# One step of a masked-attention kernel: another order, smaller TensorE tiles, other release points for the gathers

## The chip, the cores and the metric

The kernel runs on one core of a Trainium2 chip. The metric is the device time of one execution, in microseconds (us). A core has TensorE (PE; its weight loads are listed as PEld), VectorE (DVE), ScalarE (ACT), GpSimd (POOL) and SyncE (SP), each working through its own queue in order; they wait for each other on semaphores. DMA transfers are issued from SP, POOL and ACT queues.

## The reference, cut to what matters

The inputs are `x` (8 batches, 2048 nodes, 64 channels) and an integer adjacency matrix of 2048 by 2048, sparse but for the first nodes. Two graph-attention layers follow, then a leaky ReLU, a layer norm, a residual sum with `x` and a second layer norm. In one layer each node attends only to its neighbours and itself:

```python
def _gat_layer(h, mask, b):
    scores = jnp.einsum('...nd,...md->...nm', h, h)
    scores = jnp.where(mask, scores, NEG)
    attn = jax.nn.softmax(scores, axis=-1)
    return jnp.einsum('...nm,...md->...nd', attn, h) + b
...
h = jnp.einsum('bnc,hdc->bhnd', x, Wh)                      # 4 heads of 64
out_h = _gat_layer(h, mask[None, None], bh[None, :, None, :])
z = jax.nn.leaky_relu(cat, negative_slope=0.2)              # cat: heads side by side
h2 = jnp.einsum('bnk,dk->bnd', z, Wo)
out2 = _gat_layer(h2, mask[None], bo)
```

All of it is float32.

## The kernel before, in words

The first 56 nodes ("hubs") have many neighbours and are treated densely. The other 1992 nodes are split into 166 sets of 12; each set has a list of at most 128 nodes that its members are linked to. The kernel has three parts, all laid out by hand: program order is queue order on each engine.

**Hub stage** (to about 144 us). `x` is loaded, stored as `table1` in device memory, transposed by `turn_x` into `xT`, and the hubs' scores and values are computed. Meanwhile adjacency rows are loaded (`load_adj`, `raw` tiles, three buffers; reduced to 0/1 on GpSimd), turned into keys by small products (`make_keys`) and picked into neighbour lists by VectorE (`pick`, a list of jobs that the loops take one by one with `some`). The sets are listed in three rounds of 60, 60 and 46; only the first is complete when layer 1 starts.

**Layer 1** (to about 600 us) is a loop over `i`, in which one group of two sets passes through per step, each part of a step working on another group. For group `g`:
- `gather` (L792): two indirect DMAs on GpSimd's queue fetch 128 rows of `table1` each into `rows` tiles (ten buffers).
- `turn` (L512): eight TensorE transposes of 128x128 against the identity into the PSUM tile `t`; ScalarE copies `t` to `xTg`.
- `own_rows` (L800, GpSimd): own nodes' columns out of `xT`, into `xo`, every second step for two groups; `columns` (L806): `xo` times the 128x128 matrices `gram`, block diagonal with two copies of Wh^T Wh of a head; ScalarE keeps the product as `y`.
- `scores` (L821): `xTg` against `y`, in tiles of 64x64; `weigh` (L826) subtracts the mask on VectorE, `lift` (L833) is the exponential on ScalarE.
- `values` (L846): exponentials times gathered rows, with the sums of weights in an extra column; `invert` (L853, L854) divides on VectorE.
- `turn_values` (L863): four transposes of the quotients; `keep_values` (L870) copies them to `ot`.
- `project` (L531), `leaky` (L518) and `leak` (L523): the four heads' weights, bias and leaky ReLU.
- `second_maps` (L880): times Wo; `keep_own` (L885, L886) stores the result as `own`; `second_rows` (L890) transposes it, and `keep_rows` (L894) adds the bias and sends it to `table2`.

The PSUM tiles S, C, O and T have one buffer of two banks each. Within step `i` TensorE's order is: scores of group i+1, projection i-1, values i, maps i-2, rows i-3, columns i+4, first half of turn i+3, turned values i, second half of turn i+3. Gathers for group i+5 follow the values in program order; they wait until the values have let go of their buffers. In the first nine steps one more adjacency piece each is loaded and reduced (`more`), and VectorE works off the later rounds' selection jobs. From step 30 on, `load_own` and `add_beta` prepare `table3` (x plus beta) for the end.

**Layer 2** (to the end) starts when `table2` is complete: 42 steps `u` of four sets, with its own order: scores (L1133), values (L1165), transposed exponentials (L1144), `turn2` (which calls `turn`), hub parts (L1277, L1299), and the two norms spread over later steps on VectorE.

## Time and profile before

| | |
|---|---|
| median of 3 runs | 881.2 us (876.9, 881.2, 884.0) |
| the profiled execution | 880.76 us, of it 878.9 from first to last instruction |
| mean granted TensorE clock | 0.951 |

Busy us in stretches (start and end in us):

| stretch | part | length | PE | PEld | DVE | ACT | POOL | clock |
|---|---|---|---|---|---|---|---|---|
| 70 to 144 | hub stage | 74.0 | 54.8 | 37.9 | 57.9 | 24.2 | 21.3 | 0.93 |
| 152.1 to 197.7 | first steps of layer 1 | 45.6 | 39.7 | 34.4 | 27.7 | 24.2 | 21.0 | 0.93 |
| 219.5 to 584.8 | 71 steps of layer 1 | 365.3 | 358.9 | 325.1 | 256.7 | 241.5 | 200.8 | 1.00 |
| 600 to 645 | between the layers | 45.0 | 31.0 | 27.5 | 15.5 | 21.1 | 30.4 | 0.80 |
| 645 to 752 | layer 2 | 107.0 | 104.5 | 96.5 | 93.2 | 87.1 | 82.0 | 1.00 |

A row of a timeline gives start and length in us, engine, line of the kernel, operation, result and operands, the weights' shape on TensorE (rows*columns), result and operand sizes and a count; in brackets the idle time before it and what ended that. Float32 products take two passes on TensorE and are counted twice; transposes are counted once. Matmuls are pipelined, so lengths overlap: the time that a group takes is read from the start of one group to the start of the next.

### The profile page before, as it was taken

The page shows a single profiled execution, that of the slowest core. Times are in us where ns is not written, and L with a number is a line of the kernel's source. Part 1 is how long each engine was busy: PE and PEld are TensorE (multiplying, and loading weights), DVE is VectorE, ACT ScalarE, POOL GpSimd, SP SyncE. Part 2 cuts the span into 40 slices and gives each one's busy share as a digit, 9 for nine tenths or more (in the row PEclk, how much of TensorE's full clock was granted, in tenths as well). Part 3 has the DMA queues.
Part 4 walks back from the last instruction along what each step waited for, and adds up shares of the span by engine and source line. Part 5 has one row for each costly group of instructions (what it writes and reads, how often), then busy time and mean ns, then how long its engine had stood idle before and what let it go on. Part 6 is the DMA issues. An engine that isn't in the chain of part 4 may idle for free.

```text
span 878.9 us, 42066 instructions
## 1 busy us (share of the span) xinstructions
PE 753.0 (86%) x18437; PEld 661.2 (75%) x18437; DVE 610.1 (69%) x1369; ACT 514.4 (59%) x961; POOL 469.2 (53%) x612
## 2 busy tenths in 40 slices
PE   1896777889999999999999999992999999998730
PEld 1664456778788999988999999971899999988720
DVE  3356983568888788877555555553258999998994
ACT  2342333556556667666766667651678888886821
POOL 5654141457444555655666666503777777777300
PEclk9998998999999999999999999995999999999965
DMA  8787451355434445655566665514888888888611
GB/s 167 238 218 213 129 146 48 83 142 160 109 100 118 112 125 159 162 169 153 160 168 173 160 166 162 134 28 114 246 266 253 275 275 267 266 252 242 172 46 35
DMA packets 81794, 145.22 MB, mean 165 GB/s; under 512 B 30146, under 2 KB 46466, under 8 KB 81602
## 3 DMA queue, kind: packets, MB, share of 16 engines
q0 software_dynamic: 26720, 88.55, 36.4%
q1 hardware_dynamic: 37842, 49.65, 18.7%
q10 hardware_dynamic: 17040, 4.25, 2.6%
q8 instruction: 147, 2.41, 1.1%
q14 instruction: 45, 0.37, 0.1%
HBM read 123.91 MB, written 18.48 MB: 162 GB/s over the span
## 4 chain that ended last, share of the span: by engine, by line
PE 63%; DVE 15%; DMA 7%; ACT 5%; issue 4%; SPq 3%; POOL 2%; DVEq 0%; ACTq 0%; POOLq 0%
PE t L512 11%; PE s L821 10%; PE o L846 10%; PE cat L806 6%; PE o L863 4%; PE cat L531 4%; PE cat L880 3%; PE s L1133 3%; PE o L1165 3%; PE cat L890 2%; DMA raw<-in_adj_dram 2%; SPq L1248 2%; PE sh L1277 2%; PE e L1144 2%; DMA g<-table,index 1%
## 5 line engine op out<-in xcount | busy, mean ns | idle before, releaser
L792 POOL DMA_INDIRECT g<-table,index x332 | 334.9, 1009 | 236.1 <-PE o L846 140.2
L512 PE MATMUL t<-ident,g 128*128 128x128 f32 x1328 | 182.3, 276 | 15.6 <-DMA g<-table,index 12.7
L512 PEld LDWEIGHTS t<-ident,g 128*128 128x128 f32 x1328 | 154.8, 142 | 20.0 <-issue 14.0
L826 DVE TENSOR_TENSOR e<-s,mask 128x768 f32<-128x768 f32 x83 | 79.4, 956 | 87.4 <-PE s L821 85.4
L518 ACT ACTIVATE z<-cat,bhp 128x192 f32<-128x192 f32 x166 | 60.8, 418 | 85.0 <-PE cat L531 85.0
L846 PE MATMUL o<-g,e 128*64 128x65 f32 x2656 | 97.5, 227 | 0.0
L821 PEld LDWEIGHTS s<-y,xTg 64*64 64x64 f32 x5312 | 85.2, 134 | 13.9 <-issue 13.7
L821 PE MATMUL s<-y,xTg 64*64 64x48 f32 x5312 | 95.5, 220 | 0.0
L846 PEld LDWEIGHTS o<-g,e 128*64 128x64 f32 x2656 | 85.8, 140 | 9.8
L1320 ACT COPY xTg<-t 128x1024 f32<-128x1024 f32 x83 | 80.3, 1017 | 18.1 <-PE t L512 17.3
L1030 ACT COPY xTg<-t 128x1024 f32<-128x1024 f32 x83 | 84.0, 1012 | 2.0 <-PE t L512 2.0
L833 ACT ACTIVATE e<-e,shifts 128x768 f32<-128x768 f32 x83 | 79.2, 955 | 2.1 <-DVE e L826 1.7
L812 ACT COPY y<-cat 128x384 f32<-128x384 f32 (+1 forms) x80 | 40.7, 508 | 64.0 <-PE o L863 40.1
L597 ACT ACTIVATE e<-e,shifts 128x896 f32<-128x896 f32 x32 | 33.4, 1042 | 73.0 <-DVE e L594 52.1
L680 POOL TENSOR_SCALAR a<-raw 120x1024 bf16<-120x1024 int32 (+1 forms) x34 | 38.2, 1125 | 65.1 <-DMA raw<-in_adj_dram 38.4
L806 PE MATMUL cat<-xo,gram 128*128 128x192 f32 (+1 forms) x320 | 65.6, 328 | 0.0
L853 DVE RECIPROCAL rall<-o 64x8 f32<-64x8 f32 x166 | 34.0, 205 | 42.0 <-PE o L846 40.7
L854 DVE TENSOR_TENSOR osb<-o,rall 128x512 f32<-128x512 f32 x83 | 57.4, 692 | 2.9
L1165 PE MATMUL o<-g,es 128*32 128x65 f32 x2656 | 49.1, 226 | 5.9 <-DVE y_s L1188 4.5
L806 PEld LDWEIGHTS cat<-xo,gram 128*128 128x128 f32 x320 | 53.7, 203 | 0.3 <-issue 0.2
L1165 PEld LDWEIGHTS o<-g,es 128*32 128x32 f32 x2656 | 46.1, 113 | 7.0 <-issue 4.9
L1133 PE MATMUL s<-xTg,bd 128*32 128x128 f32 x1328 | 45.4, 277 | 6.2 <-ACT bd L1124 3.5
(177 smaller groups left out, 1369.3 us busy)
## 6 DMA issues: line engine op xcount, KB each, us to landing
raw<-in_adj_dram SPq DMA_DIRECT2D x32, 480.0 KB
table<-xb SPq DMA_DIRECT2D x22, 256.0 KB
xr_s<-table SPq DMA_DIRECT2D x21, 256.0 KB
g<-table,index POOLq DMA_INDIRECT x332
table<-x SPq DMA_DIRECT2D x16, 260.0 KB
x<-in_x_dram ACTq DMA_DIRECT2D x32, 128.0 KB
table<-rowt SPq DMA_DIRECT2D x166, 24.4 KB
xb<-in_x_dram SPq DMA_DIRECT2D x164, 24.0 KB
```

What stands on the lines that cost most here:

```text
L512: nc.tensor.transpose(tp[:, q * P:(q + 1) * P], rows[:, q, 1:1 + P], ident)
L518: nc.scalar.activation(z[:, hp], cat[:, :, hp * n:(hp + 1) * n], AF.Identity, bias=bhp[:, hp:hp + 1], scale=1.0)
L792: nc.gpsimd.indirect_dma_start(out=t.rearrange("n q c -> n (q c)"), out_offset=None, in_=table, in_offset=bass.IndirectOffsetOnAxis(ap=ind ...
L806: nc.tensor.matmul(cat[:, k, 2 * GM:2 * GM + n], gram[:, g % 2 * 2 + k, :], held["x", g // 2][:, :n], start=True, stop=True)
L821: nc.tensor.matmul(sp[half(r), p, (q * 2 + j) * M:(q * 2 + j + 1) * M], xt[half(p), j, q, half(r)], y[half(p), (j * Q + q) * M:(j * Q + q ...
L826: nc.vector.tensor_tensor(e[:, :16 * M].rearrange("p (a q n) -> p a q n", a=2, q=Q), sp[:, :, :8 * M].rearrange("p a (q n) -> p a q n", q= ...
L833: nc.scalar.activation(e[:, :16 * M], e[:, :16 * M], AF.Exp, bias=shifts[:, 0:1], scale=1.0)
L846: nc.tensor.matmul(op[half(p), j, o0:o0 + K1], e[:, c0:c0 + 64], rw[j][:, q, sums(p)], start=True, stop=True)
L1030: nc.scalar.copy(t, held.pop(("tp", i + 2)))
L1133: nc.tensor.matmul(sp[q * 32:(q + 1) * 32, k, :], bd[u % 3][:, k, q, :], xt[:, s % 2, q, :], start=True, stop=True, tile_position=(0, q * 32))
L1165: nc.tensor.matmul(op[t * 32:(t + 1) * 32, f, k * W2 + p:k * W2 + p + K1], e[:, 2 * q + p, k, :], rw[:, q, sums(p)], start=(a == 0 and k = ...
L1320: nc.scalar.copy(t, tp)
```

## The change

Layer 1's step gets a new order and a longer pipeline, and several products get other tile shapes:

- **Order on TensorE** in step `i`: scores i+1, projection i-2, columns i+4, maps i-3, values i, turned values i-1, rows i-4, turn i+3. The loop has one more pass. The results move to other PSUM tiles: columns beside the values (O), maps into T, turned values and rows into C.
- **Tiles.** A transpose of 128 rows becomes two of 64 rows each (`turn`, in all three parts of the kernel; `second_rows`), and the turned values' four become eight of 48 rows; the two of a pair write different PSUM banks. `columns` uses the two 64x64 blocks of `gram` in four row and column halves of TensorE instead of the block-diagonal matrix. For this, `own_rows` lays the columns out so that half of them swap partition halves: one GpSimd copy becomes three, two of which (new L812) go from one partition half to the other.
- **Gathers.** Four groups ahead instead of five; the first of a pair waits for the end of this step's scores, the second for the middle of this step's values, through dependencies given by hand. `load_adj` stands between them in the steps that have it; the copy into `own` (`store_own`), `own_rows` and `add_beta` stand behind the second.
- **VectorE.** Each selection job is split in two halves, and the counts per step go with it: six in the hub stage and in the steps before 0, three to step 15, then two. The place of `weigh`, `leak`, `invert` and of the jobs in the queue changes with the order above.
- `load_own` and `add_beta` run from step 10 on, two rounds in six steps.
- Layer 2's scores read the turned rows in two pieces of 64, as `turn` lays them out now.

In the built program's order on GpSimd, the first of the two swapping copies waits for the semaphores of all gathers that stand ahead of it in the queue.

```diff
-    def turn(tp, rows):
+    def turn(tp, rows, j=0):
         for q in range(Q):
-            nc.tensor.transpose(tp[:, q * P:(q + 1) * P], rows[:, q, 1:1 + P], ident)
+            c0 = (j * Q + q) * 64
+            for r in range(2):
+                nc.tensor.transpose(tp[:, r, c0:c0 + 64], rows[half(r), q, 1:1 + P], ident[half(r), half(r)])
...
-    def gather(table, s, layer, new):
+    def gather(table, s, layer, new, behind=None):
...
+        if behind is not None:
+            tc.add_manual_dep(g.ins, behind.ins.name, mybir.DependencyInfo(mybir.DependencyClass.Sync, mybir.DependencyReason.DATA),
+                              reason="the gather's turn")
...
     def own_rows(m):
-        w = min(4, NS - 4 * m)
         t = held["x", m] = work.tile([P, 2 * GM], F32, tag="xo", name=f"xo{m}", bufs=2)
-        src = xT[:, :, HUB:].rearrange("c q (k s) -> c s q k", s=NS)[:, 4 * m:4 * m + w]
-        nc.gpsimd.tensor_copy(t[:, :w * 48].rearrange("c (s q k) -> c s q k", s=w, q=Q), src)
+        v = t.rearrange("c (b s q k) -> c b s q k", b=2, s=2, q=Q)
+        src = xT[:, :, HUB:].rearrange("c q (k s) -> c s q k", s=NS)
+        nc.gpsimd.tensor_copy(v[:, 0], src[:, 4 * m:4 * m + 2])
+        b0 = min(4 * m + 2, NS - 2)
+        for r in range(2):
+            nc.gpsimd.tensor_copy(v[half(r), 1], src[half(1 - r), b0:b0 + 2])
-    def columns(g, cat):
-        n = min(4, NS - 4 * (g // 2)) * 48
+    def columns(g, op):
+        t = held["x", g // 2]
         for k in range(2):
-            nc.tensor.matmul(cat[:, k, 2 * GM:2 * GM + n], gram[:, g % 2 * 2 + k, :], held["x", g // 2][:, :n], start=True, stop=True)
+            for r in range(2):
+                for p in range(2):
+                    nc.tensor.matmul(op[half(p), r, Q * OW + k * GM:Q * OW + (k + 1) * GM], gram[half(r), g % 2 * 2 + k, half(r)],
+                                     t[half(r), (p ^ r) * GM:((p ^ r) + 1) * GM], start=True, stop=True)
...
-    def turn_values(g, op):
-        osb = held.pop(("o", g))
+    def turn_values(g, pt):
+        osb = held.pop(("o", g)).rearrange("a j q c -> a (j q c)")
         for w in range(4):
-            nc.tensor.transpose(turned(op)[:, w, :], osb[:112, w].rearrange("a s c -> a (s c)"), ident[:112, :112])
+            for p in range(2):
+                mine = slice(p * 64, p * 64 + M)
+                at = nc.tensor.transpose(pt[:, p, w * M:(w + 1) * M], osb[mine, w * P:(w + 1) * P], ident[mine, mine])
...
-    LOOK = 5
-    for g in range(LOOK - 2):
+    LOOK = 4
+    for g in range(3):
...
-    for i in range(-4, NG + 3):
+    for i in range(-4, NG + 4):
...
+        scored = scores(i + 1, sp) if 0 <= i + 1 < NG else None
...
+        coming = i + LOOK if i > 0 else i + LOOK + 1 if -2 <= i < 0 else NG
+        if coming < NG:
+            gather(table1, 2 * coming, 1, rows_tile, scored)
+        op = one(f"o{i}", "O")
+        if 0 <= i + 4 < NG + NG % 2:
+            columns(i + 4, op)
...
+            more(1)
...
+        if 0 <= i - 3 < NG:
+            second_maps(i - 3, tp[:, 0, :GM])
+            keep_own(i - 3, tp[:, 0, :GM])
+        midway = values(i, op) if 0 <= i < NG else None
+        if coming < NG:
+            gather(table1, 2 * coming + 1, 1, rows_tile, midway)
+        if 0 <= i - 3 < NG:
+            store_own(i - 3)
+        if i + 6 < NG and i % 2 == 0 and i >= -2:
+            own_rows((i + 6) // 2)
...
+        if 0 <= i - 1 < NG:
+            turn_values(i - 1, cat[:, :, 2 * GM:4 * GM])
+        if 0 <= i - 4 < NG:
+            second_rows(i - 4, cat[:GM, :, 384:448])
...
         if 0 <= i + 3 < NG:
-            turn(tp[:, 1, :], rows[1, 2 * (i + 3) + 1])
+            held["tp", i + 3] = tp
+            for j in range(2):
+                turn(tp, rows[1, 2 * (i + 3) + j], j)
```

## The prediction

> **What bounds the kernel now.** I read the busy shares first, then the slices, then stretches of the main stage, then one of its steps instruction by instruction. From the page, section 1 and the TensorE rows of the slices:

> ```profile
> PE 753.0 (86%) x18437; PEld 661.2 (75%) x18437; DVE 610.1 (69%) x1369; ACT 514.4 (59%) x961; POOL 469.2 (53%) x612
> ...
> PE   1896777889999999999999999992999999998730
> ...
> PEclk9998998999999999999999999995999999999965
> ```

> TensorE is full from about 200 to 595 us and again from 640 to 810 us, at the full granted clock. The two stretches (start and end, length, then the busy time of PE, PEld, DVE, ACT and POOL with counts, granted clock, DMA share, GB/s):

> ```profile
> 219.50:584.80 365.30, 358.89 (x9738) 325.08 (x9737) 256.68 (x658) 241.53 (x497) 200.76 (x265) 1.00 0.52 141
> ...
> 645.00:752.00 107.00, 104.51 (x2575) 96.53 (x2574) 93.15 (x165) 87.11 (x153) 82.02 (x83) 1.00 0.87 266
> ```

> The first is layer 1's loop. Its scores start every 4.997 us in most steps; 71 steps take 365.3 us, so 10.5 us of it are extra time in a few steps (the key products, the slot tables). One step on TensorE, by start and length:

> ```profile
> 485.35 1.15 PE L821 MATMUL s<-y,xTg 64*64 64x48 f32 x64
> 486.31 0.53 PE L531 MATMUL cat<-otb,whT 64*64 64x96 f32 x16
> 486.77 1.15 PE L846 MATMUL o<-g,e 128*64 128x65 f32 x32
> 487.75 0.50 PE L880 MATMUL cat<-z,woT 128*64 128x96 f32 x8
> 488.19 0.31 PE L890 MATMUL cat<-ident,own 128*96 128x128 f32 x1
> 488.34 0.82 PE L806 MATMUL cat<-xo,gram 128*128 128x192 f32 x4
> 488.99 0.60 PE L512 MATMUL t<-ident,g 128*128 128x128 f32 x4
> 489.43 0.55 PE L863 MATMUL o<-ident,osb 112*128 112x112 f32 x4
> 489.81 0.60 PE L512 MATMUL t<-ident,g 128*128 128x128 f32 x4
> 490.34 0.86 PE L821 MATMUL s<-y,xTg 64*64 64x48 f32 x44
> ```

> No row shows idle time: the step is the sum of its TensorE slots. Start to start: scores 0.96, projection 0.46, values 0.98, maps 0.44, rows 0.15, columns 0.65, turn 0.44, turned values 0.38, turn 0.53, together 4.99 us. The two turns are alike, but the second stands ahead of an instruction with another tile shape and takes 0.09 more; I count 0.10 for each change of tile shape. Without one, a 128-column transpose costs 0.44/4 = 0.11.

> GpSimd holds the gathers:

> ```profile
> 488.09 0.97 POOL L792 DMA_INDIRECT g<-table,index  x1 [1.94 <-PE o L846]
> 489.37 1.05 POOL L792 DMA_INDIRECT g<-table,index  x1 [0.30 <-DMA xb<-in_x_dram]
> 490.43 1.28 POOL L928 TENSOR_TENSOR xb<-xb,bet 128x512 f32<-128x512 f32 x1
> 491.65 0.26 POOL L886 COPY own<-own 128x96 f32<-128x96 f32 x1
> 493.09 0.98 POOL L792 DMA_INDIRECT g<-table,index  x1 [1.18 <-PE o L846]
> ```

> It waits for the end of the values and has 1 to 2 us to spare in each step. The trace's landing events put a gather's data 3.55 us (median of the first of each pair, 213 to 590 us) and 4.03 us (the second) after its start, up to 5.5. They are wanted more than a step later: hidden.

> **The change on TensorE.** Scores, projection, maps and values keep their passes: 0.96, 0.36, 0.34 and 0.98 without shape changes. The columns become 16 passes of 64x64 weights by 96 columns, the very form of the projection: 0.36 for 0.65. The 128-row transposes become pairs of 64-row ones. No row of this trace shows such a pair. Nearest rows: in the scores, weights on both row halves and both column halves go through four at a time, 64 passes in 0.96, 0.015 each, against 0.030 each for the values, which use all rows and overlap only two column halves; so two row halves do run side by side. From below a pair costs one full transpose (0.11), from above two (0.22). [...] I take 0.11, since the scores are the same engine in the same step. Turns: 8 pairs, 0.88, as now (8 x 0.11). Turned values: 4 pairs, 0.44 for 0.38. Rows: one pair, 0.11 for 0.15. Three shape changes remain in the step (columns to maps, values to turned values, turns to scores): 0.30. Sum: 0.96 + 0.36 + 0.36 + 0.34 + 0.98 + 0.44 + 0.11 + 0.88 + 0.30 = 4.73. The start of the values just behind a shape change is in their 0.98 already, and the projection's four rounds alone start 0.082 apart (0.33), so 4.60 is the lower end; I take 4.66, **0.34 less per step**.

> [...] No run here shows the pair yet.

> **The other engines in the step.** ScalarE: copy 1.01, two activations 0.73, exponential 0.96, columns 0.51, turned values as one 384-wide copy, about 0.51 for 0.54: 3.7 of 4.66, and no TensorE instruction waits for a copy of its own step any more. VectorE: weigh 0.96, own 0.25, leak 0.55, inverse 0.42 + 0.69, rows 0.28: 3.15, plus two half-jobs of the selection (0.42 + 0.50) 4.07; three of them before step 16 make 4.5, close but under. These hide; if ScalarE's chain slipped by half a microsecond, the maps would wait for the turned tile's copy.

> **GpSimd is where I see the new bound.** The first gather now waits for the end of the scores, the second for half the values, and with five sets in flight become four, both are wanted one step later. That alone fits: second gather at about 3.0 of the step, landed at 7.0, turned at 4.66 + 4.1. But the copy of own columns is now three copies, of which two swap the partition halves. In the built order, the first swapping copy waits for the landing of every gather issued so far, the one just issued included; in the kernel before, no copy waits for a gather. Behind it in GpSimd's queue are the next step's gathers. So every second step has a chain: landing 4.03, two copies of 64x96 (nearest row 128x96, 0.25: 0.50), gap 0.17, gather 0.98, gap 0.30, gather 1.04, own copy 0.25, gap 0.17, gather 0.98, gap 0.30, and the next second gather starts: 8.72 us per two steps, and 10.00 where the beta addition (1.28) stands in it, which is two of three pairs from step 10 to 76. Mean 9.57, against 9.32 for TensorE. Landings over the median add to the chain and those below do not give it back, so I take 4.80 per step instead of 4.66: gain 0.20 x 71 = **-14 us**. Bounds: -24 (chain hidden) and +7 (landings 0.6 later, 0.3 per step).

> SyncE's queue takes the own-node loads (eight DMAs of 24 KB) from step 10 instead of 30, two rounds in six steps; behind them stand the stores of finished rows, which have four buffers: 0, with what it does to the landings inside the bounds.

> **Early steps** (scores 152 to 219 us, 11 steps). In the first nine, the load and reduction of an adjacency piece stands between the two gathers; before, it stood behind both. The waits L680 <- raw are 7.4 us over three times here. Minus 11 x 0.34, plus about four waits of 1.5 us ahead of a second gather: **+2** (-4 to +12).

> **End of the stage.** One more pass of the loop, but the last values no longer stand behind their own step's transposes; before, 15.2 us pass from the last scores to the last rows with PE at 10.7. **-2** (-3 to +3).

> **Layer 2.** Its turns become pairs between full-height transposes, so one more shape change in each of 41 steps that TensorE fills (104.5 of 107 us): 41 x 0.10 = **+4** (0 to +8). The scores read their operand in two pieces; L880 reads pieces too, at no visible cost. The hub stage: the same turns, hidden, 0. Splitting the selection's jobs in two keeps their order: 0.

> **Sum.** -14 + 2 - 2 + 4 = -10. The profiled execution took 880.76 us (span 878.9), 0.4 below the median 881.2 of three runs that lie from 876.9 to 884.0: 880.8 - 10 = 870.8, and I say **870**. About 1% is what a measurement of this kernel can tell from no change.

> **Rivals.**
> 1. The swapping copies' wait is covered (landings nearer 3.5, since the pair is spread): steps of 4.62 to 4.66, -24 to -27 instead of -14: 847 to 860. For it: when GpSimd is on time the two gathers start 1.66 apart and not 1.28. Against it: the two-step chain, 0.25 over TensorE's. Chance 0.22.
> 2. The landings grow instead: the chain beats the old 9.99 per pair as soon as they are 0.42 later than 4.03, and the early steps pay 2 us each as well. No gain to a loss: 884 to 900. Landings of 6 to 8 us do occur between 172 and 203 us, beside the adjacency loads. Chance 0.18.
> 3. Slower, clearly: half-height transposes do not overlap. Place: turns and turned values. Price: 12 x 0.11 = 1.32 per step of layer 1, less 0.34: 83 x 0.98 = 81; 16 x 0.11 x 41 = 72 in layer 2, less than nothing elsewhere: about 1030. It decides from 0.14 per pair on, where the 0.34 is used up (12 pairs). Against it: the scores' 0.015 per pass. Chance 0.13.
> 4. My forecast, 860 to 884: 0.45; 0.02 left over.

> The range 848 to 900 holds 1, 2 and 4 but for their ends. Faster by over 1% (below 872): nearly all of 1 and some 0.28 of 4, 0.49. Within 1%: 0.17 of 4 and a little of 2, 0.23. Slower: 0.28.

> **What would show it.** Turn slots of about 0.44 per four pairs and columns of 0.36 confirm the TensorE sum. In the waits, GpSimd's swapping copy <- DMA g with 2 to 3 us in each second step, and the turn <- DMA g on TensorE in short pieces, confirm the chain; a step of 4.66 without them is rival 1; turn slots of 0.88 per four pairs are rival 3. I am wrong altogether if ScalarE or VectorE ends the waits of the step.

## The result, and the profile after

The changed kernel is **slower**: 932.3 us in the median of four runs (930.4 to 939.8), against 879.8 us for the kernel before on the same chip. The ratio is 1.061, with a 95% interval of 1.053 to 1.069. The profiled execution took 939.75 us, the slowest of the four, of it 937.9 us from first to last instruction; before it was 880.76 and 878.9. The 59 us between the two profiled executions (52.5 between the medians) lie here (start of each part read from TensorE's first scores or turns in it):

| part | before, us | after, us | difference | forecast |
|---|---|---|---|---|
| hub stage, to the first scores of layer 1 | 152.1 | 158.2 | +6.0 | 0 |
| first 11 steps | 67.3 | 75.9 | +8.6 | +2 |
| 71 steps | 365.3 | 391.8 | +26.5 | -14 |
| end of the stage, to layer 2's first turn | 26.2 | 27.0 | +0.8 | -2 |
| layer 2 | 267.8 | 285.1 | +17.2 | +4 |

The busy shares and TensorE's slices of the page, after:

```profile
PE 712.2 (76%) x21252; PEld 611.8 (65%) x21252; DVE 608.6 (65%) x1369; ACT 567.9 (61%) x878; POOL 494.2 (53%) x696
...
PE   2876687776888888888888888882887888888630
...
PEclk9997787889899999999999999995889999999975
```

TensorE has 2815 passes more (and as many weight loads) and 41 us less to do. It is not full any more in any slice: in the kernel before it was, through most of the 71 steps and in layer 2. The two stretches that answer to those shown before (start and end, length, busy time of PE, PEld, DVE, ACT and POOL, granted clock, DMA share, GB/s):

```profile
234.05:625.85 391.80, 335.84 (x11499) 299.89 (x11495) 246.23 (x623) 285.32 (x424) 222.61 (x338) 0.97 0.48 134
690.00:800.00 110.00, 90.79 (x2686) 80.18 (x2690) 85.75 (x151) 78.25 (x136) 77.22 (x76) 0.96 0.80 239
```

In the 71 steps TensorE's busy time fell from 358.9 to 335.8 us, 0.33 per step, about what the forecast said (0.34); the time that its passes need fell by more, as the step below shows. Its idle time rose from 6.4 to 56.0 us. So the question is what it waits for. The waits between 234 and 626 us, by what was waiting and what ended it (total, times, longest):

```profile
POOL xo L812 <- DMA g<-table,index: 105.0, 34, 4.5
DVE rall L873 <- ACT y L827: 65.9, 68, 2.9
...
PE t L514 <- DMA g<-table,index: 20.3, 22, 2.1
...
PE cat L537 <- DVE rowt L917: 13.1, 36, 1.1
...
PE o L863 <- issue: 6.2, 9, 1.6
PE t L897 <- DVE keys L716: 5.3, 2, 2.7
```

Three things hold TensorE: gathers that come late (20.3 us; the first line is the swapping copy on GpSimd that makes them late), a chain that ends at the projection (13.1 us), and "issue", 14.9 us over all its lines, where it waited for nothing that the profile shows. The key products' 5.3 us were there to be paid by any order.

One step without a late gather, TensorE's rows:

```profile
481.90 1.15 PE L838 MATMUL s<-y,xTg 64*64 64x48 f32 x64
483.38 0.56 PE L537 MATMUL cat<-otb,whT 64*64 64x96 f32 x16 [0.34 <-DVE rowt L917]
483.76 0.51 PE L820 MATMUL o<-xo,gram 64*64 64x96 f32 x16
484.20 0.55 PE L897 MATMUL t<-z,woT 128*64 128x96 f32 x8
484.58 1.10 PE L863 MATMUL o<-g,e 128*64 128x65 f32 x32
485.62 0.45 PE L882 MATMUL cat<-ident,osb 48*128 48x48 f32 x8
485.90 0.23 PE L913 MATMUL cat<-ident,own 64*96 64x64 f32 x2
485.96 0.66 PE L514 MATMUL t<-ident,g 64*128 64x64 f32 x16
486.55 0.33 PE L838 MATMUL s<-y,xTg 64*64 64x48 f32 x8
```

Start to start it takes 4.65 us, and 0.51 of that is waiting in the slot of the scores, 1.48 where 0.97 were needed before. So the passes alone need 4.14 us. The projection has to wait for a chain that starts when the values end: ScalarE copies the columns (0.86 us), VectorE's inverse waits for that copy (the two read different columns of the PSUM tile O), then come inverse (0.42), quotients (0.69) and rows (0.28), and only then is tile C free for the next projection. On ScalarE and VectorE:

```profile
485.73 0.87 ACT L827 COPY y<-o 128x384 f32<-128x384 f32 x1 [0.17 <-PE o L863]
```

```profile
481.98 0.42 DVE L873 RECIPROCAL rall<-o 64x8 f32<-64x8 f32 x2 [1.73 <-ACT y L827]
482.44 0.69 DVE L874 TENSOR_TENSOR osb<-o,rall 128x512 f32<-128x512 f32 x1
483.05 0.28 DVE L917 TENSOR_TENSOR rowt<-cat,bob 96x128 f32<-96x128 f32 x1
```

**The stops.** The "issue" rows look harmless one by one. Here is one in layer 2, in the middle of 64 equal passes, none of which waits for a semaphore:

```profile
710.00 0.96 PE L1194 MATMUL o<-g,es 128*32 128x65 f32 x51
713.13 0.42 PE L1194 MATMUL o<-g,es 128*32 128x65 f32 x13 [2.17 <-issue]
```

```profile
q8 instruction: 147, 2.41, 1.1%
...
q8 instruction: 168, 2.75, 1.2%
```

The times of these transfers show the wait itself. In 119 of 123 blocks of the 71 steps and layer 2, after, one transfer starts while the block runs, 1.3 us (71 steps) or 1.6 us (layer 2) after the block's begin in the median, and it takes 1.0 us. Of the 37 stops of over 0.4 us at the ends of these blocks, 36 end 1.1 to 1.65 us after the end of a transfer, and so do the only two of the kernel before (1.3 us). Where TensorE did not stop, the last transfer had ended 1.9 us (71 steps) and 3.0 us (layer 2) earlier in the median, before 2.6 and 3.0. So I read the stops as waits for the next block of instructions.

That TensorE can outrun the supply shows in the time that the blocks take. For each block I took the time between its two ends and subtracted the stop at its end (over 0.25 us from start to start); the rest is the block's own work. Blocks whose end falls on a wait for a semaphore are left out:

| kernel, part | own work of a block, us | blocks | stopped | mean stop, us |
|---|---|---|---|---|
| before, 71 steps | 3.7 to 4.2 | 10 | 1 | 0.1 |
| | over 4.2 | 63 | 0 | 0.0 |
| after, 71 steps | under 3.4 | 17 | 14 | 0.67 |
| | 3.4 to 4.2 | 44 | 12 | 0.20 |
| | over 4.2 | 22 | 1 | 0.02 |
| before, layer 2 | over 4.2 | 40 | 1 | 0.03 |
| after, layer 2 | under 3.8 | 5 | 5 | 1.79 |
| | 3.8 to 4.6 | 19 | 9 | 0.33 |
| | over 4.6 | 19 | 2 | 0.08 |

The stops sum to 19.5 us in 27 of 90 blocks of the 71 steps (0.4 before) and 16.9 in 16 of 46 in layer 2 (1.2 before). A stopped block took 4.28 us in the median in layer 1 and 5.14 in layer 2: that is the pace of the supply when it is late, some 60 and 50 instructions per us. Before, a step had 274 instructions in 5.0 us, 55 per us, and two units of layer 2 had 512 in 10.5 us, 49 per us: just below. After, it is 324 in the 4.65 us of a step without a late gather, 70 per us, and 576 per two units, 55 per us at the old pace. In layer 2 the stops alone are the loss: 17.2 us longer, 15.7 us more of stops.

So the theories to be told apart were: **A**, the supply of instructions holds the kernel; **D**, the swapping copies' wait for gathers; **G**, the chain over the columns' copy; **B**, something else of the order that layer 2 pays for.

### The profile page after: what moved, and what is told of

Same layout as the page of the kernel before. It is cut to its first block, busy times and chain, and to the rows that moved or that the text cites. A ratio compares the mean times of both kernels' runs of the same rounds, so it can differ in the third digit from the quotient of the medians.

```text
span 937.9 us, 47605 instructions
## 1 busy us (share of the span) xinstructions
PE 712.2 (76%) x21252; PEld 611.8 (65%) x21252; DVE 608.6 (65%) x1369; ACT 567.9 (61%) x878; POOL 494.2 (53%) x696
## 4 chain that ended last, share of the span: by engine, by line
PE 30%; DMA 20%; DVE 19%; issue 11%; ACT 9%; POOL 6%; SPq 3%; ACTq 0%; POOLq 0%; DVEq 0%
DMA g<-table,index 15%; PE o L863 4%; PE s L838 4%; PE t L514 3%; PE s L1162 3%; ACT y L827 2%; PE cat L537 2%; POOL g L798 2%; PE t L897 2%; PE o L1194 2%; PE sh L1306 2%; SPq L947 2%; POOL a L688 2%; PE o L820 1%; DVE keys L716 1%
## 5 line engine op out<-in xcount | busy, mean ns | idle before, releaser
L514 PE MATMUL t<-ident,g 64*128 64x64 f32 x2656 | 120.1, 232 | 55.6 <-DMA g<-table,index 48.5
L514 PEld LDWEIGHTS t<-ident,g 64*128 64x128 f32 x2656 | 100.8, 143 | 70.7 <-DMA g<-table,index 37.1
L838 PE MATMUL s<-y,xTg 64*64 64x48 f32 x5312 | 107.0, 229 | 3.2 <-issue 2.4
L863 PE MATMUL o<-g,e 128*64 128x65 f32 x2656 | 98.5, 226 | 6.2 <-issue 6.2
L1047 ACT COPY xTg<-t 128x1024 f32<-128x1024 f32 x83 | 86.4, 1041 | 27.2 <-PE t L514 26.7
L838 PEld LDWEIGHTS s<-y,xTg 64*64 64x64 f32 x5312 | 95.3, 143 | 10.3 <-issue 3.1
L1349 ACT COPY xTg<-t 128x1024 f32<-128x1024 f32 x83 | 80.6, 1016 | 27.9 <-PE t L514 25.4
L863 PEld LDWEIGHTS o<-g,e 128*64 128x64 f32 x2656 | 91.9, 142 | 8.3 <-issue 7.9
L812 POOL COPY xo<-xT 64x96 f32<-64x96 f32 x84 | 31.2, 372 | 122.8 <-DMA g<-table,index 117.9
L827 ACT COPY y<-o 128x384 f32<-128x384 f32 x80 | 69.0, 863 | 43.4 <-PE o L863 40.8
L888 ACT COPY otb<-cat 128x384 f32<-128x384 f32 x83 | 72.5, 873 | 3.4 <-PE cat L913 3.3
L537 PE MATMUL cat<-otb,whT 64*64 64x96 f32 x1328 | 51.3, 266 | 19.0 <-DVE rowt L917 17.2
L1162 PE MATMUL s<-xTg,bd 128*32 128x128 f32 x1328 | 47.3, 281 | 13.9 <-ACT bd L1153 10.2
```

Of the source, the lines that this page charges most:

```text
L514: nc.tensor.transpose(tp[:, r, c0:c0 + 64], rows[half(r), q, 1:1 + P], ident[half(r), half(r)])
L537: at = nc.tensor.matmul(cat[half(j), s, hp * n:(hp + 1) * n], whT[half(s), h * D:(h + 1) * D], ot[half(s), h, :], start=True, stop=True)
L827: nc.scalar.copy(held["y", g // 2].rearrange("p (b n) h -> p b h n", b=2)[:, :, h0:h0 + 2, :], op[:, :, Q * OW:Q * OW + 2 * GM].rearrange( ...
L838: at = nc.tensor.matmul(sp[half(r), p, (q * 2 + j) * M:(q * 2 + j + 1) * M], xt[half(p), r, j, q, :], y[half(p), c0:c0 + M], start=True, s ...
L863: at = nc.tensor.matmul(op[half(p), j, o0:o0 + K1], e[:, c0:c0 + 64], rw[j][:, q, sums(p)], start=True, stop=True)
L888: nc.scalar.copy(ot.rearrange("c h (p m) -> c p m h", p=2), pt.rearrange("c p (m h) -> c p m h", h=H))
```

## The experiments

The parts of the profiled runs on chips on which the kernel before takes about 880 us, but for the one with half of layer 2's gathers; in brackets the stops at block ends in them:

| kernel | hub stage | 11 steps | 71 steps | layer 2 | ratio to before |
|---|---|---|---|---|---|
| before | 152.1 | 67.3 | 365.3 (0.4) | 267.8 (1.2) | |
| changed | 158.2 | 75.9 | 391.8 (19.5) | 285.1 (16.9) | 1.061 (1.053 to 1.069) |
| whole turns in layer 2 | 158.0 | 75.2 | 393.8 (34.6) | 272.4 (1.1) | 1.053 (1.048 to 1.058) |
| before, half turns | 151.9 | 65.7 | 373.1 (3.3) | 273.4 (9.4) | 1.019 (1.014 to 1.025) |
| columns as before | 155.1 | 71.0 | 370.5 (13.5) | 276.7 (8.4) | 1.033 (1.026 to 1.039) |
| swaps on VectorE | 163.0 | 74.6 | 383.2 (39.1) | 277.8 (12.8) | 1.051 (1.045 to 1.057) |
| before, extra passes in layer 2 | 152.5 | 66.7 | 365.5 (0.7) | 301.2 (19.5) | one run |
| columns' copy last | 159.2 | 70.3 | 387.1 (27.8) | 279.3 (14.5) | 1.044 (1.036 to 1.052) |
| before, pairs behind the values | 153.2 | 65.8 | 388.9 (21.9) | 266.8 (0.0) | 1.020 (1.017 to 1.023) |
| selection's jobs whole | 151.2 | 74.6 | 388.4 (9.2) | 276.5 (11.5) | 1.046 (1.043 to 1.049) |
| mixed | 151.3 | 72.2 | 355.5 (9.0) | 269.0 (1.3) | 1.001 (0.998 to 1.004) |

**Whole turns in layer 2.** The edit gives layer 2 its 128-row transposes back:

```diff
-                turn(tp, rows[2, 2 * g + j], j)
+                turn_whole(tp, rows[2, 2 * g + j], j)
```

> The changed kernel, with the turns of layer 2 alone as whole 128-row transposes again (16 instructions in place of 32 per unit of two tiles); layer 1 and the hub stage keep the pairs. Theory A, supply of instructions: in the trace of the changed kernel TensorE stands still inside runs of equal passes, without a wait, and nearly every such stop lies exactly 256 TensorE instructions, or a multiple of that, behind the one before; in layer 2 the stops are 16.9 us in 16 of 46 blocks, against 1.2 us in one of 41 before. With a sixteenth to an eighth fewer instructions the stops in layer 2 fall under 2 us, layer 2 goes from 285 back to 268 us, and the whole from 932 to 915. Theory B, the new order of layer 1 leaves something late that layer 2 pays for: layer 2 stays at 285, the whole at 930. Theory C, a pair simply costs more than a whole transpose: layer 2 returns to 268 as well, but the turns of the changed kernel would have to be longer, and they were 1.2 us against 1.75 there.

Layer 2 went from 285.1 to 272.4 us and its stops from 16.9 to 1.1. B is out for layer 2. The changed kernel's 285.1 is the longest of five runs with the same layer 2 (276.5 to 285.1 in the table above, 8.4 to 16.9 of stops); less their stops all five take 265 to 268 us, and the kernel before 266.6, so the stops are what differs. The whole gained less than forecast: 928.2 us, not 915, where the kernel before took 882.9 beside it. Layer 1, whose code was not touched, had more stops than in the changed kernel's run, 34.6 us in 47 blocks, at the same length of 71 steps, and its turns waited 14.8 us for gathers, not 20.3. In the run with the selection's jobs whole, below, layer 1's steps are untouched too: 9.2 us of stops, 28.2 of late gathers, 388.4 in all. So in these steps stops and late gathers take each other's place, and with the same code the stops can differ by 25 us from run to run.

**Half turns in the kernel before.** Only `turn` and what reads its tile:

```diff
-            nc.tensor.transpose(tp[:, q * P:(q + 1) * P], rows[:, q, 1:1 + P], ident)
+            c0 = (j * Q + q) * 64
+            for r in range(2):
+                nc.tensor.transpose(tp[:, r, c0:c0 + 64], rows[half(r), q, 1:1 + P], ident[half(r), half(r)])
```

> The kernel before, with nothing changed but the turns: pairs of 64-row transposes in all three stages, and the scores read them so. Theory A (supply of instructions): layer 2 goes from 268 to 285 us with stops at block ends of 256 instructions; layer 1's step asks for 290 instructions in 4.7 us, 62 per us, at the edge of what came through in the changed kernel (a block in about 4.2 us when late, 61 per us): 4.75 to 4.9 us per step, so 71 steps in 340 to 355 in place of 365. In all 875 to 890. Theory B (the order is at fault): layer 2 stays at 268, layer 1 gains 0.3 x 71 = 21, in all 860.

897.5 us, above both forecasts. Layer 2 has stops (9.4 us in 10 of 47 blocks) without anything of the new order: A's sign, at half its size. But the 71 steps became 7.8 us longer with only 3.3 us of stops. Neither theory had that. One step of it:

```profile
485.77 0.82 PE L813 MATMUL cat<-xo,gram 128*128 128x192 f32 x4
486.52 0.46 PE L514 MATMUL t<-ident,g 64*128 64x64 f32 x8
486.91 0.60 PE L870 MATMUL o<-ident,osb 112*128 112x112 f32 x4
487.44 0.46 PE L514 MATMUL t<-ident,g 64*128 64x64 f32 x8
487.83 0.27 PE L828 MATMUL s<-y,xTg 64*64 64x48 f32 x4
```

Inside a run the pairs start 0.061 us apart, little more than half of a whole transpose (0.109), not the same. But where a 64-row run meets a 128-row one, 0.26 us lie between the last start of the columns and the first of the turn (0.16 with whole turns), 0.15 behind the turn and 0.19 behind the turned values (0.11 and 0.10), and the second pair, or transpose, of a run comes 0.05 us later than the next ones. A change of shape costs 0.1 to 0.15 us in all, and the old order has three more of them with half turns. The median step is 5.05 us, 5.00 before. Here the changes take back what the pairs save.

**Columns as before.** One GpSimd copy instead of three, four passes with 128x128 weights, and a copy on ScalarE with neighbouring elements:

```diff
-            for r in range(2):
-                for p in range(2):
-                    nc.tensor.matmul(op[half(p), r, Q * OW + k * GM:Q * OW + (k + 1) * GM], gram[half(r), g % 2 * 2 + k, half(r)],
-                                     t[half(r), (p ^ r) * GM:((p ^ r) + 1) * GM], start=True, stop=True)
+            nc.tensor.matmul(op[:, k, Q * OW:Q * OW + n], gram[:, g % 2 * 2 + k, :], held["x", g // 2][:, :n], start=True, stop=True)
```

> The changed kernel, with the columns alone as they were: four passes of 128x128 weights in place of sixteen of 64x64, one copy of the own columns on GpSimd in place of three, the columns' copy on ScalarE over 192 neighbouring elements. Theory D, the swapping copies' wait for the gathers holds layer 1 (GpSimd waited 105 us there, TensorE's turns 20 us for gathers): the 71 steps go from 391.8 to about 360, with TensorE's sum 0.29 longer per step than 4.65. Theory A: 24 instructions fewer of some 324 per step; the stops at block ends, 19.5 us in layer 1, fall to about half, so 391.8 to 380 by that alone. Both together about 350, and the whole at 932 - 40 = 890. Layer 2 stays at 285 by both.

A ratio of 1.033, the most that one part gave back. The 71 steps took 370.5 us. The waits of the turns for gathers are gone from TensorE's list, the scores' slot is 1.14 instead of 1.48 (the columns' copy takes 0.52 us in the mean, not 0.86), and the stops fell to 13.5 us, with 24 instructions fewer per step. What D, G and A name went down together; this run does not separate them.

**Swapping copies on VectorE**, where they wait for no gather:

```diff
-            nc.gpsimd.tensor_copy(v[half(r), 1], src[half(1 - r), b0:b0 + 2])
+            nc.vector.tensor_copy(v[half(r), 1], src[half(1 - r), b0:b0 + 2])
```

> The changed kernel, with the two swapping copies of the own columns on VectorE, where they do not wait for gathers. Theory D (their wait holds layer 1): GpSimd's 105 us of waiting for gathers go, TensorE's 20 us at the turns with them; 71 steps from 391.8 to 368, the whole at 908. Theory A (supply of instructions holds it): the steps come closer together, the stops at block ends grow from 19.5 to 30 us or more, and half of that gain is given back: 380, the whole at 920. Theory E, VectorE was already the bound (two copies of 0.2 to 0.4 us more per two steps): no gain, 390, the whole at 930.

This is the forecast's own suspect, taken away alone, and the ratio falls by one percent, to 1.051. In the 71 steps TensorE waits for no gather any more. The largest of its waits now:

```profile
PE cat L537 <- DVE rowt L917: 12.9, 38, 0.7
PE o L863 <- issue: 12.2, 13, 2.2
PE s L838 <- issue: 8.4, 12, 1.5
```

The stops doubled, 39.1 us in 52 of 90 blocks, more than in any run with layer 1 untouched (9.2 to 34.6): of the 20.3 us of late gathers, 8.6 were gained, and late instructions took their place, as A had it.

**The columns' copy last in the step**, behind the inverse and the turned values' copy:

```diff
-        if 0 <= i + 4 < NG + NG % 2:
-            keep_columns(i + 4, op)
         if 0 <= i < NG:
             invert(i, op)
...
         if 0 <= i - 4 < NG:
             keep_rows(i - 4, cat[:GM, :, 384:448])
+        if 0 <= i + 4 < NG + NG % 2:
+            keep_columns(i + 4, op)
```

> The changed kernel with the columns' copy issued last in a step, again. Where the kernel before takes about 880 us: theory A (60 instructions per us, 324 per step) keeps the 71 steps at 380 to 392 us, with 30 us or more of stops at block ends in place of the projection's waits; theory G (the chain over that copy holds the step) brings them to 355 to 367.

The chain went: the scores' slot is 0.97 us again. The 71 steps are 387.1 us, and the stops 27.8 in 42 blocks. G alone would have given 355 to 367 and is out; A's length holds. That the chain's time came back as stops is not shown: 27.8 us lies within what unchanged steps had, and 19.9 us of late gathers are there as well. The shortest of its four executions took 14 us less than the profiled one; even with all of that taken from the 71 steps, 373 us stay. The same edit on two other chips is told of below.

**Extra passes in the kernel before.** Whole turns, the old order, and in layer 2 sixteen more products per unit, one column each, into columns that nothing reads:

```diff
+            for t in range(4):
+                nc.tensor.matmul(op[t * 32:(t + 1) * 32, 1, 4 * W2 + k:4 * W2 + k + 1], e[:, t, k, :], rw[:, 0, 1:2], start=False, stop=False,
+                                 skip_group_check=True, tile_position=(0, t * 32))
```

> The kernel before with sixteen more one-column products in each unit of layer 2, again. Where the kernel before takes about 880 us: by TensorE's time alone layer 2 goes from 268 to 288 us without stops; by theory A (a block of 256 instructions takes some 5.1 us in layer 2 when it is late, 640 instructions per two units) to 300 to 315 with 15 us or more of stops at block ends.

Layer 2 took 301.2 us and had 19.5 us of stops in 16 of 51 blocks, at places such as these, in the middle of passes that the edit did not touch:

```profile
643.42 0.39 PE L1302 MATMUL oh<-gh,esh 120*64 120x65 f32 x5 [2.29 <-issue]
...
719.31 1.80 PE L512 MATMUL t<-ident,g 128*128 128x128 f32 x15 [1.10 <-issue]
```

That settles the cause for layer 2: the number of instructions does it, without half-height passes. The rest of the 33 us, 15, is less than the 20 that the passes were priced at.

**Half of layer 2's gathers** left out of the changed kernel (a tile with an odd number reads the rows of the one before it):

```diff
+        if s % 2 == 0:
+            gather(table2, s, 2, rows2)
+        else:
+            rows[2, s] = rows[2, s - 1]
```

> The changed kernel with every second gather of layer 2 left out (a tile with an odd number reads the rows of the tile before it; a long second way follows at the end and is not read), again. First to last scores of layer 2 take 231 us in the changed kernel. If the blocks come late because they share the DMA engines with the gathers: stops under 4 us in that stretch, 215 to 220 us. If the supply has a limit of its own: 8 us or more of stops, 225 us or more.

From the first to the last scores of layer 2 it took 217.2 us, as the first case said, but with 7.6 us of stops in 10 of 44 blocks, between the two. The DMA share in this stretch was 0.51 in place of 0.78. The stops do not go, and that they got fewer by it is not shown, since the same layer 2 with all gathers had as few as 8.4 us; how the two share the engines stays open. The 13.9 us gained are more than the 9.3 of stops.

**Both half turns behind the turned values**, in layer 1 of the kernel before, so that the 64-row passes stand together:

```diff
-        if 0 <= i + 3 < NG:
-            tp = held["tp", i + 3] = one(f"t{i + 3}", "T")
-            turn(tp[:, 0, :], rows[1, 2 * (i + 3)])
         if 0 <= i < NG:
             turn_values(i, op)
             keep_values(i, op)
         if 0 <= i + 3 < NG:
-            turn(tp[:, 1, :], rows[1, 2 * (i + 3) + 1])
+            tp = held["tp", i + 3] = one(f"t{i + 3}", "T")
+            for j in range(2):
+                turn_two(tp, rows[1, 2 * (i + 3) + j], j)
```

> The kernel before with both turns of layer 1 as half-height pairs behind the turned values, again. On the slow chip its passes showed what was not in the sum: the turned values now follow the columns at once and wait 0.35 us for the inverse of the values, so that TensorE's step is 5.00 us again, as before (0.93 + 0.50 + 0.93 + 0.49 + 0.99 + 0.53 + 0.64). So now 5.0 per step, 71 steps in 363 to 370, the whole within 1% of the kernel before; 348 to 356 and 865 to 873 if that wait was the slow chip's alone.

A miss on both sides: 896.4 us. The steps are 5.0 us, for the reason given (weight loads wait for the quotients, first line), but 21.9 us of stops came on top in 21 of 81 blocks:

```profile
PEld o L870 <- DVE osb L861: 20.8, 61, 1.1
PEld o L853 <- issue: 17.7, 17, 1.9
```

Ten of the 21 stopped blocks had own work of 4.2 to 4.6 us; in the last kernel below only one such block of 29 stopped. 290 instructions in 5.0 us should nearly have passed, but turns, scores and projection now follow each other with 192 of them in 1.9 us. Whether these bursts are the reason is not shown.

**The selection's jobs whole** in the hub stage, three at a time, as before:

```diff
-            some(6)
+            some(3)
```

> The changed kernel, with the jobs of the first selection round whole and three at a time in the hub stage, as before; layer 1's rounds stay split. Theory H (VectorE's bursts of six half jobs, of which the closing ones are not half, delay the hub stage's subtractions): start to first scores of layer 1 from 158 back to 152 us, the whole from 932 to 926. Rival: the split is worth nothing and the hub stage's 6 us come from the loads of the adjacency, which TensorE waits for in both kernels: 156 to 160 us, no difference.

The hub stage is 151.2 us, as theory H said, and the whole 920.2. Yet the last kernel, below, keeps the split jobs and has 151.3, with whole turns there. Split jobs with half turns gave 155 to 163 in six kernels, either of the two alone 151 to 152. So the 6 us need both; how they do it is open.

**Mixed**: the changed kernel with whole turns in the hub stage and layer 2, columns as before, and the columns' copy last. Its edits are those shown.

> The changed kernel with whole turns in the hub stage and layer 2, columns as before (four passes, one GpSimd copy) and the columns' copy last in the step: 300 TensorE instructions per step. By the blocks measured: a block's own work is 256/300 of TensorE's sum, 4.62, so 3.9 us, where blocks of 3.8 to 4.2 us stopped for 0.14 to 0.21 us in the mean: a step of 4.85, 71 of them 345, and some 20 us for key products and late gathers, 365. Hub stage 155, early steps 71, tail 26, layer 2 at 270: 887 of span, the same as before within 1.5%. If the supply played no part in layer 1: steps of 4.62, 71 in 345, the whole at 866.

879.8 us, a ratio of 1.001. The windows of the 71 steps and of layer 2:

```profile
223.47:579.01 355.54, 340.67 (x10656) 301.52 (x10652) 250.03 (x628) 259.23 (x426) 206.21 (x267) 0.99 0.52 146
607.80:876.84 269.04, 215.42 (x5248) 196.37 (x5248) 209.52 (x381) 180.22 (x319) 161.47 (x161) 0.91 0.71 215
```

The 71 steps are 9.8 us shorter than before; the median step is 4.63 us. The 11 early steps, where the turns still wait for gathers (7.3 us), and the end of the stage give 7.5 back. So the new order with half turns in layer 1 is worth about 10 us in these steps, and no version was faster than the kernel before.

**Two groups of runs on other chips.** Eight runs fell on two chips on which the kernel before took 1041 to 1045 us and TensorE paused for 0.6 us and more inside runs of passes, away from block ends. Six of them had four of the edits above. The ratios were 1.072 and 1.059 for the columns' copy last (one on each chip) and 1.011 for the pairs behind the values; half the gathers ran twice and is not compared. The extra passes made no difference there, against the forecast of 300 to 315 us for layer 2: 1040.1 us in one run against 1041.3. Layer 2 took 399 us with them, so a block had 7.8 us, and the stops at block ends were some 5 us. With the columns' copy last they were some 6 us in all, so the supply is not what makes that kernel 6 to 7% slower on those chips; what does, beside the pauses, is open. Two edits were tried there alone. Scores with 64x128 weights, half as many passes:

```diff
-                    for r in range(2):
-                        at = nc.tensor.matmul(sp[half(r), p, (q * 2 + j) * M:(q * 2 + j + 1) * M], xt[half(p), r, j, q, :],
-                                              y[half(p), c0:c0 + M], start=True, stop=True)
+                    at = nc.tensor.matmul(sp[:, p, (q * 2 + j) * M:(q * 2 + j + 1) * M], xt[half(p), j, q, :],
+                                          y[half(p), c0:c0 + M], start=True, stop=True)
```

> The changed kernel, with layer 1's scores as products with 64x128 weights in place of pairs of 64x64: 32 passes for 64 in a step, and the copy of the turned tile on ScalarE puts the two halves side by side for it. TensorE's time should stay: 16 half-height transposes, the same tile shape, start 0.027 us apart, so 32 passes take 0.88 us, against 0.89 for the 64 now; one shape change moves from ahead of the scores to behind them. But a step has 260 TensorE instructions in place of some 324. Theory A (supply of instructions, about one block of 256 in 4.2 us in layer 1): the stops at block ends in the 71 steps (19.5 us in the changed kernel, 34.6 and 39.1 in two of its variants) fall under 4 us; the 71 steps go from 392 to 370 or less, the whole from 932 to 910. Rival F, the stops only stand in the place of another wait (the chain over the columns' copy, the gathers), and come back as that: 71 steps in 385 to 392, the whole at 925 to 932.

The ratio is 1.089, and the price was wrong by a factor of two: a row pair of such float32 products takes 0.111 us, where a pair of transposes takes 0.061, so the scores took 1.7 us in place of 0.93. The supply of instructions was not tested by it. Nor by this one, which had the same scores in it, besides columns with 128x64 weights and whole turns outside layer 1:

> The changed kernel's order with few TensorE instructions: whole turns in the hub stage and layer 2, half-height turns in layer 1 alone, wide scores, columns as four products with 128x64 weights (one GpSimd copy of the own columns, columns and maps then have one shape), the columns' copy last in the step. About 244 TensorE instructions per step (before: 274, changed: 324), TensorE's sum some 4.3 us, ScalarE's 4.1 to 4.5. Theory A: no stops worth naming, steps of 4.4 to 4.8, so 71 steps in 315 to 345 (before 365), layer 2 at 268, the whole at 840 to 870, faster than both. If the supply of instructions is not what held the changed kernel: 71 steps over 370, the whole at 890 or more.

Its ratio is 1.020 (1.016 to 1.024).

## Why the prediction was wrong

It said 870 us and faster; it was 932 and slower, outside the range. What failed is not the price of the passes, which need even less time than it said, but the overlap: it let TensorE wait for one chain alone, at 0.14 us per step, and put ScalarE, VectorE and the supply of instructions at nothing. In the 71 steps TensorE stood idle for 56.0 us, not 6.4: 20.3 for gathers, 13.1 behind the columns' copy, 14.9 at "issue", 14.6 of it at block ends; in layer 2 such stops were 15.7 us more. By its own steps:

- **TensorE's sum per step** (4.66, which is 0.34 less): half a microsecond too long. The slots without the wait come to 4.14 us. The 0.11 per pair of 64-row transposes, taken there as the least that a pair could cost, was an estimate that no run shows: a pair cost 0.061 us. The turns took 0.59 of the step and not 0.98 with their change of shape, the turned values 0.29 and not 0.54. Changes of shape were priced at 0.10 and cost 0.1 to 0.15. That busy time fell by 0.33 us per step, as forecast, is luck: passes that run out before a wait still count as busy (the scores' row above is 1.15 us long, 0.93 from first to last start), and so do passes at half the clock.
- **"These hide"** for ScalarE and VectorE: this step failed. The columns' copy was priced at 0.51 us and took 0.86 with its new layout, and the forecast didn't ask what else reads its tile. The inverse waits for that copy, and the projection for the rows behind it: 0.34 us of idle time in the step shown, 13.1 us in 36 waits. The text names this as what would make it wrong ("if ScalarE or VectorE ends the waits of the step").
- **GpSimd's chain**: the mechanism is there, 105 us in 34 waits (3.1 each; 2 to 3 were named). Its price per step, 0.14, was under the 20.3 us that TensorE waited, 0.29 per step. But taken away, it gave back only 8.6 us of the 71 steps and one percent of the whole.
- **Early steps** +2: +8.6, inside the bounds of -4 to +12; the turns wait 12.8 us for gathers there. **End of the stage**: +0.8 against -2, inside.
- **Layer 2** +4 (0 to +8): the step that failed most clearly. It was costed by a shape change; the 16 half transposes more per unit were not counted as instructions. The stops are 15.7 of its 17.2 us.
- **Hub stage** and **split jobs**, both 0: +6.0, from the two together.
- **The rivals.** The premise of the slow one (half-height transposes do not overlap) is refuted by 0.061 per pair. The one with growing landings has its sign (medians of 3.86 and 4.29 us between 234 and 625 us, 3.55 and 4.03 before), and its range ended at 900. None had the supply of instructions. The count that leads to it, 274 instructions in a step of 5.0 us and 324 in one of 4.66, follows from the passes that the forecast counted.

The granted clock fell as well: in the 71 steps it was at half in eight stretches of 3.4 us or longer, 13.7 us of lost clock in all, and not once before. The kernels with few waits in those steps (before, and before with half turns) have none (1.00 in these steps); that the waits bring the half clock about is not shown. The intervals between TensorE's starts that fall into these eight stretches, without a wait or a block end in them, are together 9 us longer than the same intervals at the full clock; how much of that the whole would gain without them is open.

## What to carry to other kernels

Count TensorE's instructions per us before splitting its passes: here 55 per us passed in layer 1, and a block that stopped there took 4.28 us in the median, 60 per us; in layer 2, with more transfers beside it (a DMA share of 0.80, not 0.48), 49 per us passed and 55 did not. So a split that saves TensorE time can still lose. When one of several waits of a step is removed, look for the next in line first; here three (late gathers, a copy's chain, late instructions) stood behind each other, and the gathers and the chain, taken away alone, gave back less than they showed. Before a wait is read as grown or shrunk by an edit, look how much it differs between runs with the same code: here the stops of the 71 steps did by 25 us. Put tiles of one shape together, since a change between 64-row and 128-row passes costs as much here as about two pairs of half transposes.

## What the runs showed that I had not expected

- TensorE stops at block ends of 256 instructions when a block's own work is under about 3.4 us in layer 1 (14 of 17 blocks) or 3.8 us in layer 2 (5 of 5), and for up to 2.4 us.
- A stop ends 1.1 to 1.65 us after the end of a transfer of 16 KB of instructions (36 of 37 stops); one such transfer starts in nearly every block (119 of 123).
- Two 64-row transposes side by side take 0.061 us, one with 128 rows 0.109; two 64-row float32 products with 128 columns take 0.111.
- A change between 64-row and 128-row passes costs 0.1 to 0.15 us.
- Chips differ: the kernel before took 877 to 883 us on two of them and 1041 to 1045 on two others, where layer 2 took about 400 us (402.8 in a kernel with the layer 2 of before).
